# A transformer block on one core: when the output projection's operand and weights are loaded beside attention

## The chip, the cores and the metric

The kernel runs on one core of a Trainium2 chip. A core has TensorE (PE, matrix products; its weight loads are listed as PEld), VectorE (DVE), ScalarE (ACT), GpSimd (POOL) and SyncE (SP), which here only issues DMA transfers. The metric is the time on the device of one execution, in microseconds; lower is better.

## The reference

One block with adaptive layer norm, for 2 sequences of 1024 tokens with 1024 features. Shifts, scales and gates come from a product of `silu(c)` with `wmod`.

```python
h = _layernorm(x) * (1 + ca) + sa
qkv = clip(h @ Wqkv.T, -8, 8)                      # q and k get a layer norm of their own
scores = q k^T * scale + slope_h * (key - query)   # 32 heads of 32, causal
out = softmax(scores) @ v
x = x + ga * (out @ Wout.T)
h = _layernorm(x) * (1 + cb) + sb
x = x + gb * (((silu(h @ Wg.T * ag)) * (h @ Wu.T * au)) @ Wd.T * ad)   # inner size 2752
```

## The kernel before

**Seven products.** Every large product is done in 2 x 2 blocks by a scheme with seven block products and sums of blocks. `SEVEN` (L780) lists them in order, with the index `e` from 0 to 6:

| e | product | left operand | weights |
|---|---|---|---|
| 0 | P1 | A11 | B11 |
| 1 | P2 | A12 | B21 |
| 2 | U2 | S2 | T2 |
| 3 | P5 | S1 | T1 |
| 4 | U3 | S3 | T3 |
| 5 | P53 | S4 | B22 |
| 6 | U6 | A22 | T4 |

A11, A12, A21 and A22 are blocks of the left operand, S1 to S4 their sums (S1 = A21 + A22, S2 = S1 - A11, S3 = A11 - A21, S4 = A12 - S2). B are blocks of the weights and T sums of them, which an earlier part of the kernel has computed and stored. One product is four matmul instructions; the trace has two records for each.

**Attention in groups.** Attention goes through 32 groups `GROUPS` (L1044): batch `b`, half `qb` of the queries, and `k`, four heads. Groups 0 to 15 are batch 0, 16 to 31 batch 1. Each has 4 (`qb` = 0) or 8 (`qb` = 1) units, one for each block of 128 keys. `chunk` (L1056) loads a group's queries `cq`, keys `ck` and values `cv` on SP's queue; there are two buffers of each, so `cq` and `ck` wait until TensorE has done with the scores of the group two before and `cv` until it has done with that group's product with the values (`weigh`, L1113). `scores` makes the scores `sc`, ScalarE their exponentials `p`, GpSimd masks them, VectorE and GpSimd add them up for the row sums. At the end of a group `weigh` stores the result `ao` (L1130), and `settle` (L1137) the row sums `sum` (L1154); after the last group of a half the reciprocals `rec` are stored.

**Dense work beside it.** `together` (L1198) runs attention as one generator and the dense work as another and decides by estimated times which one records its next instructions. TensorE's order is that recorded order (`pinned`). The other queues, SP's among them, are ordered by a scheduler, subject to the dependencies that the kernel adds by `behind` (an instruction stands after another one in the queue). While attention of batch 1 runs, the dense work is the output projection, `output` (L1318), for the blocks (b, j) of 256 tokens: (0,0) to (0,3), (1,0), (1,1), and after the end of attention (1,2) and (1,3).

**The operand.** `operand` (L1260) makes the left operand of one block in steps, each ending in a `yield`. Step 1 issues eight loads on SP: four `rb` (the reciprocals of the row sums, each row spread over 32 partitions, L1268) and the four blocks A11, A12, A22, A21 (`aoA<-ao`, L1284). Step 2 multiplies A22 and A21 by `rb`, step 3 A11 and A12 and makes S1, step 4 makes S2 and S3, step 5 makes S4. A11, A22, S1 and S2 are made on VectorE, A12, A21, S3 and S4 on GpSimd. `ahead` (L1342), called between the products of one block, starts the next block's operand at `e` = 2 and takes one more step at each of `e` = 3, 4, 5 and 6:

```python
if e == 2 and nxt not in made and not step and (nxt[0], 2 * nxt[1] * P // QB) in settled:
    step[0], step[1] = operand(*nxt, ap_), e
    next(step[0])
elif e > 2 and step and e > step[1]:
```

**The output weights.** `weights_b` (L800) loads B11 and B21 at once; the five others, T2, T1, T3, B22 and T4 (`wT_o`, `wB_o`), are put in the list `later`, and `ahead` issues them two products before their use: `while later and 7 - len(later) <= e + 2`.

**After a block.** Each product's bank is evicted by ScalarE or VectorE (`oP`, `oU`), gated and added to `xr` on GpSimd, normalised, transposed by TensorE (L751), evicted by VectorE as `h2t` (L871), summed into `tT` and stored as `hs` for the feed-forward stage, which follows after about 1350 us. All transposes and the row sums of `settle` use one and the same bank, so a transpose waits for the `h2t` evictions of the one before.

Of the kernel before, what the change touches and what calls it, by code (L numbers as in the profile page):

```python
# [19 lines left out]
P = 128  # L20
H = 32
HD = 32
# [458 lines left out]
def kernel(  # L481
# [19 lines left out]
    nc = tc.nc  # L501
# [183 lines left out]
    def behind(ins, first):  # L685

        tc.add_manual_dep(
            ins.ins, first.ins.name,
            mybir.DependencyInfo(mybir.DependencyClass.NoSync, mybir.DependencyReason.DATA),
            reason="behind",  # L690
        )

    last_exp = [None]
    last_chunk = [None]
    chain_copy = [None]
    last_mask = [None]
    beside = [False]

    def masked(ins):
        if beside[0]:  # L700
            behind(ins, last_mask[0])
        return ins
# [344 lines left out]
    def attention(pools, adders, banks):  # L1047
# [8 lines left out]
        def chunk(i):  # L1056
            if i < len(GROUPS) and i not in chunks:
                b, qb, k = GROUPS[i]
                while (b, qb) not in ready:
                    yield None  # L1060
                n = (qb + 1) * QB
                qc = chp.tile([P, QB], FP, tag="cq", name=f"cq_{b}_{i}")
                kc = chp.tile([P, S], FP, tag="ck", name=f"ck_{b}_{i}")
                vc = chp.tile([P, NT, P], FP, tag="cv", name=f"cv_{b}_{i}")
                nc.sync.dma_start(qc, qk_dram[b][0][:, k, ds(qb * QB, QB)])
                nc.sync.dma_start(kc[:, 0:n], qk_dram[b][1][:, k, 0:n])
                last_chunk[0] = nc.sync.dma_start(vc[:, 0 : n // P], v_dram[b][:, 0 : n // P, ts(k, P)])
                chunks[b, qb, k] = chunks[i] = (qc, kc, vc)

        def scores(b, qb, k, jb):  # L1070
            qc, kc, _ = chunks[b, qb, k]
# [106 lines left out]
        for i, u in enumerate(UNITS + [None] * (LAG + 2)):  # L1178
# [10 lines left out]
            if i >= LAG and queue:  # L1189
                b, qb, k, jb, ps = queue.pop(0)  # L1190
# [69 lines left out]
    def operand(b, j, ap_):  # L1260


        qb, y0 = 2 * j * P // QB, 2 * j * P % QB
        at, low_, rbp = ap_
        rb = rbp.tile([P, KC, 2 * P], FP, tag="rb", name=f"rb_{b}_{j}")
        nk = KC - 1 if (b, qb, KC - 1) == GROUPS[-1] else KC
        for g in range(4):
            nc.sync.dma_start(  # L1268
                rb[ts(g, HD), 0:nk],
                rec_dram[b][qb].rearrange("(k g) q -> g k q", g=4)[g][0:nk, ds(y0, 2 * P)].partition_broadcast(HD),  # L1270
            )
        if nk < KC:
            nc.scalar.copy(rb[:, nk], right["last"][:, ds(y0, 2 * P)])
        a = {
            q: (low_ if q in ("A22", "S1", "S2", "S4") else at).tile(
                [P, KC // 2, P], FP, tag=q, name=f"ao{q}_{b}_{j}", bufs=2 if q in ("A21", "A22") else None,
            )
            for q in ("A11", "A12", "A21", "A22", "S1", "S2", "S4")
        }
        blocks = (  # L1280
            (0, 0, "A11", nc.vector), (0, 1, "A12", nc.gpsimd), (1, 1, "A22", nc.vector), (1, 0, "A21", nc.gpsimd),
        )
        for m, kh, q, eng in blocks:
            nc.sync.dma_start(a[q], ao_dram[b][qb][:, ds(kh * 4, 4), ds(y0 + m * P, P)])  # L1284
        yield

        def scaled(q):
            m, kh, eng = next((m, kh, eng) for m, kh, q_, eng in blocks if q_ == q)
            ins = eng.tensor_mul(a[q], a[q], rb[:, ds(kh * 4, 4), ts(m, P)])
            if eng is nc.gpsimd:  # L1290
                masked(ins)

        scaled("A22")
        scaled("A21")
        yield
        scaled("A11")
        nc.vector.tensor_add(a["S1"], a["A21"], a["A22"])
        scaled("A12")
        yield
        nc.vector.tensor_sub(a["S2"], a["S1"], a["A11"])  # L1300
        a["S3"] = a["A21"]
        masked(nc.gpsimd.tensor_sub(a["S3"], a["A11"], a["A21"]))
        yield
        masked(nc.gpsimd.tensor_sub(a["S4"], a["A12"], a["S2"]))
        made[b, j] = a
        yield

    def operands(b, j, *args):
# [5 lines left out]
    gates = {}  # L1314

    later = []

    def output(b, js, pools, banks, bt, todo, keep, q0=3, after=None):  # L1318

# [8 lines left out]
        for j in js:  # L1328
# [5 lines left out]
            for m in range(2):  # L1334
                xr = tkp[j % 2].tile([P, D], FP, tag="xr", name=f"xr_{b}_{qts[m]}")
                nc.sync.dma_start(xr, x[b, ts(qts[m], P), :])
                xs.append(xr)
            part_t = {}
            step = {}
            nxt = (b, j + 1) if j + 1 < NJ else (b + 1, 0)  # L1340

            def ahead(e):  # L1342


                while later and 7 - len(later) <= e + 2:
                    later.pop(0)()
                if e == 2 and nxt not in made and not step and (nxt[0], 2 * nxt[1] * P // QB) in settled:
                    step[0], step[1] = operand(*nxt, ap_), e
                    next(step[0])
                elif e > 2 and step and e > step[1]:  # L1350
                    step[1] = e
                    next(step[0])

            def read(q, bank):
                if q in ("P1", "U2", "P5"):
# [313 lines left out]
    if True:  # L1669
# [180 lines left out]
        with ExitStack() as dn:  # L1850
# [22 lines left out]
            def load(dst, src):  # L1873
                ins = nc.sync.dma_start(dst, src)
                if loads:
                    behind(ins, loads[-1])
                loads.append(ins)
# [141 lines left out]
```

## Time and profile before

| | us |
|---|---|
| median of 3 runs | 2265.51 |
| the 3 runs | 2265.51, 2263.86, 2270.93 |
| profiled execution | 2262.51 |
| its span, first to last instruction | 2260.7 |
| TensorE busy in it | 2143.8 |
| mean granted TensorE clock | 0.984 |

All rows of the profile are from that one execution, with times in microseconds from the start of the span. A row of the timeline gives start, duration, engine, line, operation, output <- inputs and shape, with equal instructions that follow each other merged; the brackets give the idle time of the engine before it and what ended it. Names have no buffer numbers: `aoA` is any of the blocks A, `aoS` any sum, `wT_o` any of the output weights T. A row of the waits gives who waited for whom, then total, number of times and longest. `SPq` is SP's queue: its rows are the issue of transfers, not their course. The profile gives no landing time of transfers; where a landing is named, it is the time at which a wait for it ended.

### The profile page before, as it was taken

The page shows a single profiled execution, that of the slowest core. Times are in us where ns is not written, and L with a number is a line of the kernel's source. Part 1 is how long each engine was busy: PE and PEld are TensorE (multiplying, and loading weights), DVE is VectorE, ACT ScalarE, POOL GpSimd, SP SyncE. Part 2 cuts the span into 40 slices and gives each one's busy share as a digit, 9 for nine tenths or more (in the row PEclk, how much of TensorE's full clock was granted, in tenths as well). Part 3 has the DMA queues.
Part 4 walks back from the last instruction along what each step waited for, and adds up shares of the span by engine and source line. Part 5 has one row for each costly group of instructions (what it writes and reads, how often), then busy time and mean ns, then how long its engine had stood idle before and what let it go on. Part 6 is the DMA issues. An engine that isn't in the chain of part 4 may idle for free. (4 is left out here: it accounts for less than half of the span.)

```text
span 2260.7 us, 27238 instructions
## 1 busy us (share of the span) xinstructions
PE 2143.8 (95%) x9537; PEld 1170.8 (52%) x9537; DVE 1352.1 (60%) x1811; ACT 943.3 (42%) x1782; POOL 1098.0 (49%) x775
## 2 busy tenths in 40 slices
PE   5999999999999999899999888899998999999998
PEld 2444444333333333232222235788877888788887
DVE  5775653455566633457667676788976555534535
ACT  1222223445444445466555414554554444333331
POOL 2330112443344554586677563677977667312212
PEclk9999999999999999999999999999999999999999
DMA  9877776545425531854553366767758777598765
GB/s 370 321 288 265 293 276 240 184 145 194 168 80 199 174 116 48 281 171 140 148 168 103 100 204 205 216 206 245 251 195 256 242 228 233 202 379 314 275 225 189
DMA packets 319349, 482.44 MB, mean 213 GB/s; under 512 B 16092, under 2 KB 235036, under 8 KB 310244
## 3 DMA queue, kind: packets, MB, share of 16 engines
q1 hardware_dynamic: 316752, 472.19, 62.4%
q10 hardware_dynamic: 2452, 8.43, 1.0%
q8 instruction: 77, 1.26, 0.2%
q14 instruction: 68, 0.56, 0.1%
HBM read 323.01 MB, written 157.55 MB: 213 GB/s over the span
## 5 line engine op out<-in xcount | busy, mean ns | idle before, releaser
L1103 ACT ACTIVATE p<-sc,kw 128x128 f32<-128x128 f32 (+3 forms) x1024 | 422.1, 513 | 390.1 <-PE sc L748 365.5
L748 PE MATMUL bank<-wT,a 128*128 128x512 f32 x768 | 366.6, 611 | 14.1 <-DVE wT L834 7.9
L1135 POOL TENSOR_TENSOR p<-p,p 128x1024 f32<-128x1024 f32 (+3 forms) x128 | 263.4, 2058 | 212.8 <-PE av L748 186.0
L1135 DVE TENSOR_TENSOR p<-p,p 128x1024 f32<-128x1024 f32 (+3 forms) x192 | 242.7, 1281 | 110.8 <-POOL p L1107 68.2
L748 PE MATMUL bank<-wB,a 128*128 128x512 f32 x576 | 270.2, 605 | 1.2 <-DVE raw L993 0.6
L748 PEld LDWEIGHTS bank<-wT,a 128*128 128x128 f32 x768 | 136.8, 191 | 200.2 <-issue 167.1
L1107 POOL TENSOR_SCALAR_AFFINE_SELECT p<-p 128x256 f32<-128x256 f32 x256 | 137.1, 548 | 182.3 <-ACT p L1103 171.3
L748 PE MATMUL sc<-cq,ck 32*128 32x512 f32 (+3 forms) x1536 | 181.6, 538 | 11.7 <-DMA ck<-qk 8.4
L748 PE MATMUL av<-p,cv 128*32 128x512 f32 (+3 forms) x1536 | 168.8, 500 | 13.2 <-POOL p L1107 13.0
L748 PEld LDWEIGHTS bank<-wB,a 128*128 128x128 f32 x576 | 102.1, 189 | 141.9 <-issue 128.8
L1899 DVE TENSOR_TENSOR lo<-lo,hi 128x1408 fp32r<-128x1408 f32 x56 | 96.3, 1723 | 93.1 <-ACT hi L1898 93.1
L748 PEld LDWEIGHTS sc<-cq,ck 32*128 32x128 f32 x1536 | 61.8, 184 | 149.8 <-issue 82.4
L1898 ACT CAST hi<-lo 128x1408 fp32r<-128x1408 f32 x56 | 76.9, 1375 | 134.0 <-DMA lo<-act 89.7
L1963 POOL TENSOR_TENSOR early_P<-early_P,x1in 128x512 f32<-128x512 f32 x16 | 35.7, 2234 | 165.1 <-DVE early_P L1961 160.3
L748 PEld LDWEIGHTS av<-p,cv 128*32 128x32 f32 x1536 | 33.7, 108 | 146.5 <-issue 80.9
L1694 POOL TENSOR_TENSOR wS<-wst,wst 128x1024 fp32r<-128x1024 f32 (+1 forms) x22 | 65.9, 2997 | 87.5 <-PE uy L748 61.9
L993 DVE TENSOR_TENSOR raw<-P,bank 128x512 f32<-128x512 f32 x48 | 32.8, 684 | 119.1 <-PE bank L748 98.9
L748 PE MATMUL gx<-hs,wS 128*128 128x512 f32 (+1 forms) x352 | 90.6, 399 | 10.6 <-ACT gP L1808 7.0
L748 PE MATMUL gy<-hs,wS 128*128 128x512 f32 (+1 forms) x352 | 89.4, 396 | 9.5 <-DVE gP L1813 6.4
L748 PE MATMUL gx<-hs,wA 128*128 128x512 f32 (+1 forms) x352 | 89.0, 393 | 1.5 <-ACT h2t L873 1.5
L748 PE MATMUL uy<-hs,wS 128*128 128x512 f32 (+1 forms) x352 | 87.2, 390 | 1.2 <-DVE uP L1813 1.2
L748 PE MATMUL ux<-hs,wS 128*128 128x512 f32 (+1 forms) x352 | 88.3, 393 | 0.0
(266 smaller groups left out, 3996.3 us busy)
## 6 DMA issues: line engine op xcount, KB each, us to landing
lo<-act SPq DMA_DIRECT2D x56, 704.0 KB
a<-hop SPq DMA_DIRECT2D x20, 1792.0 KB
wm<-in_L_wmod_dram SPq DMA_DIRECT2D x48, 512.0 KB
act<-aS SPq DMA_DIRECT2D x88, 256.0 KB
wB<-in_L_attn_Wqkv_dram SPq DMA_DIRECT2D x21, 1024.0 KB
wst<-in_L_ffn_Wg_dram SPq DMA_DIRECT2D x40, 512.0 KB
wst<-in_L_ffn_Wu_dram SPq DMA_DIRECT2D x40, 512.0 KB
qk<-qs SPq DMA_DIRECT2D x16, 1024.0 KB
```

Of the source, the lines that this page charges most:

```text
L748: return in_order(nc.tensor.matmul(*args, **kw_))
L993: nc.vector.tensor_add(dst, part_t[MATE[q]], bank)
L1103: last_exp[0] = nc.scalar.activation(p[:, g, lo:hi], sp[:, g, lo:hi], AF.Exp, bias=kw[:, d, h_ : h_ + 1])
L1107: last_mask[0] = nc.gpsimd.affine_select(out=p[:, :, 0:P], in_=p[:, :, 0:P], pattern=[[0, 2], [1, P]], compare_op=ALU.is_ge, fill=0.0, bas ...
L1135: adders[b](half, jb).tensor_add(dst, dst, ps[half][:, :, 0:n])
L1694: ins = nc.gpsimd.tensor_add(f["S1"], raw["A21"], raw["A22"])
L1898: nc.scalar.copy(hi, lo.bitcast(FP))
L1899: nc.vector.tensor_sub(lo, lo.bitcast(FP), hi.bitcast(FP))
L1963: eng.tensor_add(y, y, x1_of.pop(s))
```

## The change

The eight loads of an operand are no longer issued at once but put in a list `deferred`; `flush()` issues them. It is called in `chunk` right behind a group's `cq`, `ck` and `cv`, and at the latest when `operand` goes on to its second step. While attention runs, each of these loads is put behind the last `cv` in SP's order; for the first operand (0,0), and once attention is over, they are issued at once. `chunk` also issues one of the remaining output weights, and `ahead` issues them one product before their use instead of two. The second step of `operand` is taken at `e` = 4 instead of 3 and each later one a product later; the last (S4) is taken at the start of the next block, from the list `unfinished`, and `made` is set one step earlier so that the next block finds its operand.

```diff
@@ -692,6 +692,11 @@
 
     last_exp = [None]
     last_chunk = [None]
+    deferred = []
+
+    def flush():
+        while deferred:
+            deferred.pop(0)()
     chain_copy = [None]
     last_mask = [None]
     beside = [False]
@@ -1066,6 +1071,9 @@
                 nc.sync.dma_start(kc[:, 0:n], qk_dram[b][1][:, k, 0:n])
                 last_chunk[0] = nc.sync.dma_start(vc[:, 0 : n // P], v_dram[b][:, 0 : n // P, ts(k, P)])
                 chunks[b, qb, k] = chunks[i] = (qc, kc, vc)
+                flush()
+                if later:
+                    later.pop(0)()
 
         def scores(b, qb, k, jb):
             qc, kc, _ = chunks[b, qb, k]
@@ -1264,11 +1272,6 @@
         at, low_, rbp = ap_
         rb = rbp.tile([P, KC, 2 * P], FP, tag="rb", name=f"rb_{b}_{j}")
         nk = KC - 1 if (b, qb, KC - 1) == GROUPS[-1] else KC
-        for g in range(4):
-            nc.sync.dma_start(
-                rb[ts(g, HD), 0:nk],
-                rec_dram[b][qb].rearrange("(k g) q -> g k q", g=4)[g][0:nk, ds(y0, 2 * P)].partition_broadcast(HD),
-            )
         if nk < KC:
             nc.scalar.copy(rb[:, nk], right["last"][:, ds(y0, 2 * P)])
         a = {
@@ -1280,9 +1283,25 @@
         blocks = (
             (0, 0, "A11", nc.vector), (0, 1, "A12", nc.gpsimd), (1, 1, "A22", nc.vector), (1, 0, "A21", nc.gpsimd),
         )
+
+        def load(*args):
+            ins = nc.sync.dma_start(*args)
+            if beside[0] and (b, j) != (0, 0):
+                behind(ins, last_chunk[0])
+
+        for g in range(4):
+            deferred.append(lambda g=g: load(
+                rb[ts(g, HD), 0:nk],
+                rec_dram[b][qb].rearrange("(k g) q -> g k q", g=4)[g][0:nk, ds(y0, 2 * P)].partition_broadcast(HD),
+            ))
         for m, kh, q, eng in blocks:
-            nc.sync.dma_start(a[q], ao_dram[b][qb][:, ds(kh * 4, 4), ds(y0 + m * P, P)])
+            deferred.append(
+                lambda m=m, kh=kh, q=q: load(a[q], ao_dram[b][qb][:, ds(kh * 4, 4), ds(y0 + m * P, P)])
+            )
+        if (b, j) == (0, 0) or not beside[0]:
+            flush()
         yield
+        flush()
 
         def scaled(q):
             m, kh, eng = next((m, kh, eng) for m, kh, q_, eng in blocks if q_ == q)
@@ -1300,9 +1319,9 @@
         nc.vector.tensor_sub(a["S2"], a["S1"], a["A11"])
         a["S3"] = a["A21"]
         masked(nc.gpsimd.tensor_sub(a["S3"], a["A11"], a["A21"]))
+        made[b, j] = a
         yield
         masked(nc.gpsimd.tensor_sub(a["S4"], a["A12"], a["S2"]))
-        made[b, j] = a
         yield
 
     def operands(b, j, *args):
@@ -1314,6 +1333,7 @@
     gates = {}
 
     later = []
+    unfinished = []
 
     def output(b, js, pools, banks, bt, todo, keep, q0=3, after=None):
 
@@ -1336,20 +1356,25 @@
                 nc.sync.dma_start(xr, x[b, ts(qts[m], P), :])
                 xs.append(xr)
             part_t = {}
+            for go in unfinished:
+                next(go)
+            unfinished.clear()
             step = {}
             nxt = (b, j + 1) if j + 1 < NJ else (b + 1, 0)
 
             def ahead(e):
 
 
-                while later and 7 - len(later) <= e + 2:
+                while later and 7 - len(later) <= e + 1:
                     later.pop(0)()
                 if e == 2 and nxt not in made and not step and (nxt[0], 2 * nxt[1] * P // QB) in settled:
                     step[0], step[1] = operand(*nxt, ap_), e
                     next(step[0])
-                elif e > 2 and step and e > step[1]:
+                elif e > 3 and step and e > step[1]:
                     step[1] = e
                     next(step[0])
+                    if e == 6:
+                        unfinished.append(step[0])
 
             def read(q, bank):
                 if q in ("P1", "U2", "P5"):
```

## The prediction

> **What bounds the kernel now.** I read the page first: TensorE is busy 95% of the span, so only its idle microseconds, and those at a lowered clock, can be won.
>
> ```profile
> PE 2143.8 (95%) x9537; PEld 1170.8 (52%) x9537; DVE 1352.1 (60%) x1811; ACT 943.3 (42%) x1782; POOL 1098.0 (49%) x775
> ```
>
> The change touches the stretch in which attention of batch 1 runs beside the output projection, about 915 to 1310. The waits of TensorE (here between 900 and 1345) name one large loss:
>
> ```profile
> PE av L748 <- POOL p L1107: 13.0, 8, 5.7
> PE bank L751 <- DVE h2t L871: 11.2, 9, 3.8
> PE sc L748 <- DMA ck<-qk: 8.4, 1, 8.4
> ```
>
> The stretches around it show TensorE fully idle for six microseconds and then granted half its clock:
>
> ```profile
> 934.00:940.00 6.00, 5.10 (x43) 1.50 (x42) 4.11 (x4) 3.19 (x9) 5.10 (x8) 1.00 1.11 221
> 940.00:946.00 6.00, 0.00 (x0) 0.00 (x0) 3.37 (x5) 0.00 (x0) 1.84 (x2) 0.79 1.13 293
> 946.00:952.00 6.00, 4.46 (x11) 1.72 (x12) 0.12 (x1) 2.35 (x4) 1.01 (x2) 0.50 1.03 373
> ```
>
> (Columns: length; busy PE, PEld, DVE, ACT, POOL; granted clock; DMA share; GB/s.) The timeline of SP's queue says why the keys came late: they were issued at 941.85, behind three output weights and seven transfers of the next operand.
>
> ```profile
> 920.25 0.44 SPq L820 DMA_DIRECT2D wT_o<-wt  x1
> 920.79 1.42 SPq L1130 DMA_DIRECT2D ao<-aot  x1
> 922.31 0.54 SPq L1067 DMA_DIRECT2D cv<-v  x1
> ...
> 923.73 1.94 SPq L820 DMA_DIRECT2D wT_o<-wt  x2
> 926.86 4.65 SPq L1268 DMA_DIRECT2D rb<-rec  x4
> 932.05 6.43 SPq L1284 DMA_DIRECT2D aoA<-ao  x3
> 938.96 2.30 SPq L1130 DMA_DIRECT2D ao<-aot  x1
> 941.31 0.49 SPq L1065 DMA_DIRECT2D cq<-qk  x1
> 941.85 0.50 SPq L1066 DMA_DIRECT2D ck<-qk  x1
> ```
>
> TensorE's timeline shows what follows: scores, then product P5, then U3 at 957.17.
>
> ```profile
> 947.54 2.09 PE L748 MATMUL sc<-cq,ck 32*128 32x512 f32 x8 [8.44 <-DMA ck<-qk]
> 949.56 3.78 PE L748 MATMUL bank<-wT_o,aoS 128*128 128x512 f32 x4
> 954.90 1.98 PE L748 MATMUL bank<-wT_o,aoS 128*128 128x512 f32 x4
> 957.17 1.13 PE L748 MATMUL bank<-wT_o,aoA 128*128 128x512 f32 x2
> ```
>
> **What goes.** In the built program of the changed kernel TensorE's order is the same, and cq and ck of group 19 stand before the operand, right behind T1. The 8.44 us wait goes. So does the slow clock after it: the four matmul records took 3.78 instead of 1.98 (1.80), the scores held TensorE 2.02 to the next start instead of 1.07 at 926.44 (0.95), the next values' product 0.77 instead of 0.57 (0.20). Together 8.44 + 2.95 = 11.39. By the Trainium skill (TensorE: Matmul & The Clock Gate, Part 1) an idle window of about 3.4 us halves the clock until about as long has been busy; half speed for 3.4 us would cost 1.7, the gain be 10.1. The row decides: 11.4. Without any wait U3 would start at 957.17 - 11.39 = 945.8.
>
> **What is late next: T2 and T3.** T2 stood before ao and cv of 18, now behind both. T3 stood before the operand, now behind cq, ck, two xr tiles, cv and ao of the next group and all eight operand transfers (the eighth, A21, was issued near 459 before, since nothing held it). When a transfer landed can be read where the queue itself or VectorE waits for it: second xr 928.0, T2 930.5, ao 931.2, cv 932.0, T1 by 935.0, T3 938.9, A11 943.9, A12 944.7, A22 945.4, keys 947.5. They land in the order of issue. I take from these gaps 0.7 per 256 KB (0.65 per xr half), 2.5 for T2, about 3.2 for T3 (between 2.5 and its gap of 3.9), and 4.2 for the four rb. Replayed in the new order from 928.0: ao, cv and T2 give 928.0 + 1.5 + 2.5 = 932.0, where TensorE asks at 930.93: 1.1 us of wait. T1 has the same bytes before it as now, 935.0, in time. cq and ck 936.4, needed near 940: the cure works. Two xr 939.0, cv and ao 940.4, four rb 944.6, four A 947.5, T3 950.7. TensorE asks for T3 at 945.8 + 1.1 = 946.9: 3.8 us of wait. After the 3.26 us wait at 1325.69 four records took 3.68 instead of 1.98, so 1.7 more. B22 and T4 follow behind ao, cq, ck and cv at about 956.4 and 959.2; before, P53 started 10.3 after U3, so it asks near 961 or later, T4 later still: nothing.
>
> Sum here: 11.39 - 1.1 - 3.8 - 1.7 = 4.8 us won.
>
> A rule speaks against that replay: by the Trainium skill (DMA: Bandwidth & Descriptors, Queues, rings and completion order) completion is not in order per issuing engine; a later small transfer may be complete first. If T3 passed the operand, its wait and slow clock would go and the gain be 10.3. The ten landings above are in order, so I keep 4.8 and use the other as a bound. The lower bound: T3 is issued once the first rb has landed (eight semaphores are used in turn), at 941.5 to 943.5; with its issue-to-landing of before, 938.9 - 925.4 = 13.5, it lands at 955 to 957, and next to nothing is won.
>
> **The other operands.** Loads of (0,2), (0,3), (1,0), (1,1) now start behind cv of groups 24, 26, 28 and 30 and one ao, near 1009, 1075, 1141 and 1202 on the old time axis. Eight transfers need about 7 us by the paces above, 12 at worst. Their first products start at 1039, 1100, 1171 and 1246, and their sums stand on VectorE near 1023, 1089, 1155 and 1218: at least 4 us are left. On SP they delay the group's row sums, the xr and hs transfers and the next cq and ck. The sums' single rs buffer is wanted a group later (12 to 30 us); ck of group 25, issued at 1013.46, is first used at 1062; nothing reads hs before the feed-forward stage. Nothing, then.
>
> **Moved sums, on VectorE and GpSimd.** No operation is added; four on VectorE (0.69 each) and four on GpSimd (1.27 each) per operand stand later. Where they leave, these waits shrink:
>
> ```profile
> 1021.30 0.66 PE L751 MATMUL bank<-ident,xr 128*128 128x128 f32 x4 [1.83 <-DVE h2t L871]
> 1060.48 1.12 PE L748 MATMUL bank<-wT_o,aoS 128*128 128x512 f32 x2 [2.35 <-DVE oP L1365]
> ```
>
> At 1021.30 the evictions h2t stood behind S1 and S2 (1.21 + 0.69), which go: 1.8 won. At 1060.48 oP waited behind A11 of (0,3), which itself waited 1.41 for its load: about 1.75 won. Where they arrive: for (1,0), A11 and A22 now stand among the h2t evictions that the transpose at 1157.02 waits for, 2 x 0.69 = 1.4 lost. For (1,1), A22, A11, S1 and S2 stand before an h2t that ended at 1223.24, where TensorE asks at 1224.41: 2.8 more, less 0.6 and the 1.2 of slack, and a little handed on to the 3.8 us wait at 1232.55, about 1.4 lost. For (0,3) the h2t behind them is the last of its tile, and the GpSimd masks delayed by 2.6 end near 1092 for a product at 1096.7: nothing. S4 moves to the start of the next output and is used five products later: nothing. (1,2) and (1,3) load at once as before; of (1,3) the sums slip behind one tT operation of 0.7 us, ten before their use. Net 3.55 - 2.8 = 0.75 won; both ends, none of the gains or none of the losses, are -2.8 and +3.6.
>
> **Sum.** 4.8 + 0.75 = 5.55 us. The profiled execution took 2262.51 (span 2260.7 and 1.8 around it), so it becomes 2257.0. It lies 3.0 below the median 2265.51; the same difference on the median's scale gives 2260.0, or 0.24% less. About 0.3% (6.8 us) is what can be told from no change.
>
> **Rivals.**
> - *Fully hidden.* T2 and T3 are in time: 11.4 + 0.75 = 12.1, 2253.4. For it: low traffic once the keys are out of the way, and transfers need not land in order. Against it: eight operand transfers stand directly before T3. Chance 0.22.
> - *The wait changes hands.* T3 lands at 955 to 957: U3 starts where it did, with a slow clock again; between 2 won and 4 lost, near 2266. For it: T3's 13.5 us before. Chance 0.17.
> - *Slower.* One mechanism: T3, issued at 943.5 behind eight loads at the 221 GB/s that the stretch from 934 shows while they run, lands after 961, since the 1 MB of T3 then shares with wB22 and T4 issued behind it. Landing at 964 costs 964 - 957.2 = 6.8 and 1.7 of clock above now, 2274. It decides from 957.2 upward and beats the measurement's grain from about 962. Against it: T3's bytes stand ahead of theirs. Chance 0.17, the reordered evictions going worse included.
> - *It does not do what it says.* If the keys still waited, the time would stay; the new order excludes that.
>
> **How the numbers follow.** My forecast, 2 to 8 us won, has 0.44. Faster by over 0.3%: the hidden case, 0.22, and 0.14 of the forecast's upper part, 0.36. Same: the rest of the forecast, 0.30, and the wait that changes hands, 0.17, 0.47. Slower: 0.17. The range leaves out 2 in 10: it goes down past the hidden case with all VectorE gains (11.4 + 3.6 = 15.0, 2250.5), to 2251, and up to 2271, the losses on VectorE on top of the wait that changes hands.
>
> **What would show it.** After the change no wait sc <- DMA ck near 940; clock near 1.00 there; a wait of bank<-wT_o for DMA wT_o near 947 of 3 to 4 us; T2's near 931 about 1. The waits at 1021 and 1060 are gone, those near 1157 and 1224 longer by 1.4 and 1.7. Wrong if T3 shows no wait, or one over 9 us, or if cq and ck of a later group are waited for.

## The result, and the profile after

The changed kernel takes 2272.98 us (median of 20 runs, 2263.89 to 2278.61), the kernel before, timed with it, 2263.47. The ratio is 1.0042, 95% interval 1.0033 to 1.0050: 0.42% slower, about 9.5 us. The forecast was 2260.0 with a range up to 2271. From here on every version is given by its ratio to the kernel before, each compared with runs of that kernel on the same chip; "+9.5" is (ratio - 1) x 2263. By the intervals a difference between two such numbers is uncertain by about 3 us.

The profiled execution after took 2272.35 (span 2270.5). TensorE has the same instructions, and 2.5 us more busy time; so most of what was lost is idle time. The page of the changed kernel:

```profile
PE 2146.3 (95%) x9537; PEld 1172.4 (52%) x9537; DVE 1359.2 (60%) x1811; ACT 943.3 (42%) x1782; POOL 1104.8 (49%) x775
```

The largest of its waits of TensorE between 900 and 1345, to be set against those before (lines lie five to 25 further down in the file):

```profile
PE av L753 <- POOL p L1115: 14.8, 9, 4.8
PE bank L756 <- DVE h2t L876: 13.4, 8, 4.2
PE bank L753 <- DMA wT_o<-wt: 8.9, 2, 5.5
PE bank L753 <- DVE oP L1390: 4.7, 2, 3.2
```

The 8.4 us for the keys are gone. In their place stand two waits for output weights, 8.9 together, and the waits for GpSimd's `p` and VectorE's `h2t` are 1.8 and 2.2 longer. The stretches around the old wait (length; busy PE, PEld, DVE, ACT, POOL; granted clock; DMA share; GB/s):

```profile
928.00:934.00 6.00, 2.81 (x20) 0.78 (x18) 3.04 (x4) 3.84 (x8) 5.78 (x8) 1.00 1.01 407
934.00:940.00 6.00, 5.79 (x26) 2.03 (x30) 0.69 (x1) 0.58 (x1) 1.21 (x3) 0.72 0.45 171
940.00:946.00 6.00, 6.00 (x44) 1.83 (x37) 4.47 (x4) 4.04 (x11) 4.66 (x6) 1.00 0.87 204
946.00:952.00 6.00, 4.80 (x31) 1.57 (x29) 1.74 (x3) 4.54 (x9) 2.64 (x5) 1.00 0.99 235
952.00:958.00 6.00, 1.69 (x2) 0.50 (x2) 0.69 (x1) 0.00 (x0) 0.00 (x0) 0.73 1.03 373
```

The hole at 940 is now two holes, at 930 and 952, each with a lowered clock behind it. Look at the DMA share of the second row as well: from 934 to 940, a few us before T3 is wanted, the transfer engines are less than half used. SP's timeline says why:

```profile
921.50 1.32 SPq L825 DMA_DIRECT2D wT_o<-wt  x1
...
923.54 0.58 SPq L825 DMA_DIRECT2D wT_o<-wt  x1
926.11 0.32 SPq L1070 DMA_DIRECT2D cq<-qk  x1
927.28 0.32 SPq L1071 DMA_DIRECT2D ck<-qk  x1
928.55 1.05 SPq L1356 DMA_DIRECT2D xr<-_attn_hidden_states_dram  x2
938.27 0.38 SPq L1072 DMA_DIRECT2D cv<-v  x1
938.93 0.33 SPq L1138 DMA_DIRECT2D ao<-aot  x1
939.35 2.09 SPq L1288 DMA_DIRECT2D rb<-rec  x4
941.54 5.64 SPq L1288 DMA_DIRECT2D aoA<-ao  x4
947.23 2.93 SPq L825 DMA_DIRECT2D wT_o<-wt  x1
```

T2 is issued at 921.50, T1 at 923.54, then the keys of group 19. After the second `xr` the queue stands for 8.7 us (928.55 + 1.05 to 938.27) in front of `cv` of group 19, which needs the buffer that TensorE frees with the last product of group 17 with its values. That product stands behind U2, and U2 waits for T2. TensorE's timeline:

```profile
934.21 3.65 PE L753 MATMUL bank<-wT_o,aoS 128*128 128x512 f32 x4 [3.40 <-DMA wT_o<-wt]
937.79 0.43 PE L753 MATMUL av<-p,cv 128*32 128x128 f32 x8
...
943.97 1.14 PE L753 MATMUL sc<-cq,ck 32*128 32x512 f32 x8
...
956.31 2.07 PE L753 MATMUL bank<-wT_o,aoA 128*128 128x512 f32 x2 [5.51 <-DMA wT_o<-wt]
```

U2 starts 3.28 us later than before (930.93), its four records take 3.65 at the lowered clock, and the product with the values ends at 938.2: then SP goes on. The scores of group 19 start at 943.97 without a wait, 3.57 earlier than before in spite of that. Matched instruction by instruction, TensorE is 0.2 us ahead of the kernel before at 925, 4.9 behind at 937.8, 6.4 ahead at 948, and after T3's wait and slow clock 1.6 behind at 962. The whole gain is gone there.

The rest is lost between 1100 and 1245, at three places, one for each of the operands (0,3), (1,0) and (1,1):

```profile
1101.84 1.85 PE L753 MATMUL av<-p,cv 128*32 128x384 f32 x8 [3.12 <-POOL p L1115]
...
1162.63 0.83 PE L756 MATMUL bank<-ident,xr 128*128 128x128 f32 x4 [4.19 <-DVE h2t L876]
...
1233.42 0.66 PE L756 MATMUL bank<-ident,xr 128*128 128x128 f32 x4 [1.34 <-DVE h2t L876]
```

Before, there was no wait at the first and third of these, and one of 0.61 at the second. The kernel before at the first two:

```profile
1099.17 0.85 PE L748 MATMUL av<-p,cv 128*32 128x384 f32 x8
...
1157.02 0.66 PE L751 MATMUL bank<-ident,xr 128*128 128x128 f32 x4 [0.61 <-DVE h2t L871]
```

At the first place TensorE waits for the last masks on GpSimd. They stand behind the output's work (`tT`, `oU`, `xr`), as they did before, where they were done at 1098.99, 0.2 ahead of their product:

```profile
1098.22 0.77 POOL L1107 TENSOR_SCALAR_AFFINE_SELECT p<-p 128x256 f32<-128x256 f32 x2
```

Now that work starts later. A12 and A21 of (0,3) stand in front of it on GpSimd, and even then GpSimd is idle for 1.38 until `h2t` is evicted, because on VectorE A11, A22 and S1 of the same operand (0.88, 1.43 and 0.68, from 1089.41 on) stand among the evictions:

```profile
1087.00 1.94 POOL L1308 TENSOR_TENSOR aoA<-aoA,rb 128x512 f32<-128x512 f32 x1 [0.27 <-DMA sum<-rs]
...
1089.72 1.69 POOL L1308 TENSOR_TENSOR aoA<-aoA,rb 128x512 f32<-128x512 f32 x1
...
1093.61 1.27 POOL L1241 TENSOR_TENSOR tT<-h2t 128x512 f32<-128x512 f32 x1 [1.38 <-DVE h2t L876]
...
1098.20 2.24 POOL L1242 TENSOR_TENSOR tT<-h2t,tT 128x512 f32<-128x512 f32 x1
1100.40 1.75 POOL L1115 TENSOR_SCALAR_AFFINE_SELECT p<-p 128x256 f32<-128x256 f32 x2
```

VectorE's timeline ahead of the second: A11 and A22 of (1,0) stand among the evictions, as the prediction had it, but they take 2.21 and 1.52, not 0.69 each.

```profile
1157.64 2.21 DVE L1308 TENSOR_TENSOR aoA<-aoA,rb 128x512 f32<-128x512 f32 x1
1159.77 1.04 DVE L876 TENSOR_SCALAR h2t<-bank,modt 128x128 f32<-128x128 f32 x3
1160.73 1.52 DVE L1308 TENSOR_TENSOR aoA<-aoA,rb 128x512 f32<-128x512 f32 x1
1162.17 0.40 DVE L876 TENSOR_SCALAR h2t<-bank,modt 128x128 f32<-128x128 f32 x1
```

By the shifts of TensorE against the kernel before, instruction by instruction, it is 0.7 ahead at 1080. The first place costs 5.0 (2.3 of it comes back by 1131), the second 4.4 and the third 2.4, slow clocks and smaller waits nearby included; at 1246 it is 8.9 behind.

### The profile page after: what moved, and what is told of

Read it like the earlier page. It is cut to its first block, busy times and chain, and to the rows that moved or that the text cites. A ratio compares the mean times of both kernels' runs of the same rounds, so it can differ in the third digit from the quotient of the medians.

```text
span 2270.5 us, 27209 instructions
## 1 busy us (share of the span) xinstructions
PE 2146.3 (95%) x9537; PEld 1172.4 (52%) x9537; DVE 1359.2 (60%) x1811; ACT 943.3 (42%) x1782; POOL 1104.8 (49%) x775
## 5 line engine op out<-in xcount | busy, mean ns | idle before, releaser
L1143 DVE TENSOR_TENSOR p<-p,p 128x1024 f32<-128x1024 f32 (+3 forms) x192 | 248.1, 1308 | 114.5 <-POOL p L1115 66.8
L753 PE MATMUL ux<-hs,wA 128*128 128x512 f32 (+1 forms) x352 | 87.6, 390 | 0.5 <-DVE uP L1838 0.5
```

What stands on the lines that cost most here:

```text
L753: return in_order(nc.tensor.matmul(*args, **kw_))
L1143: adders[b](half, jb).tensor_add(dst, dst, ps[half][:, :, 0:n])
```

## The experiments

Theory A says that two of the three parts lose and one wins: the late weights (W) lose because of T2's and T3's place on SP's queue, the late sums (S) because they crowd VectorE and GpSimd where evictions and masks are due, and the late loads (L) win. The rivals: the transfers ask for more than the engines can move, whatever their order (B); the late loads, not the late sums, push the operand's work into the evictions (C); gains are given back later anyway (D). In the expectations the letters are those of each text.

In every kernel below TensorE's order is the same. Profiled executions differ by up to 4 us before the stretch is reached, so places are judged by their waits and by shifts within a trace.

### One part undone, or one alone

*W undone* (no_w):

```diff
-                if later:
-                    later.pop(0)()
...
-                while later and 7 - len(later) <= e + 1:
+                while later and 7 - len(later) <= e + 2:
```

> The changed kernel with its weights issued two products ahead again (T2 in front of the stores, T3 in front of group 19's queries and keys); the loads behind the group and the later sums stay. Theory A (two separate losses: T2 and T3 come late because of where they now stand on SP's queue, and the operand's multiplications and sums crowd the evictions later on): the waits for wT_o near 931 and 951 and the slow clock behind them go, so that TensorE runs about 11 us ahead of the kernel before at 960, instead of 1 us behind; the crowding stays, about 9 to 10 us lost between 1090 and 1245. Time near 2261.5 (2258 to 2265). Rival B (T3 is late because eight operand loads and everything else share the DMA bandwidth, not because of its place): a wait for wT_o of 3 us or more stays near 950, time 2268 or more.

Measured: 1.0032 (1.0020 to 1.0045), +7.2: 2.3 less than the changed kernel. The weights' waits went as theory A had it (one of 1.6 is left, T2's), but the time did not: it lies where rival B had it, for another reason. TensorE was 11 us ahead at 953, and 3.7 ahead at 965, because the keys of the next group, 20, were late instead (times of the kernel before). SP's timeline of this kernel, and TensorE's wait:

```profile
948.00 1.37 SPq L821 DMA_DIRECT2D wB_o<-in_L_attn_Wout_dram  x1
949.47 0.66 SPq L1136 DMA_DIRECT2D ao<-aot  x1
950.23 1.28 SPq L1070 DMA_DIRECT2D cq<-qk  x1
951.56 0.44 SPq L1071 DMA_DIRECT2D ck<-qk  x1
```

```profile
957.48 2.09 PE L753 MATMUL sc<-cq,ck 32*128 32x512 f32 x8 [5.49 <-DMA ck<-qk]
```

The wait moved one group on: the keys of group 20 stand behind the eight operand loads and behind B22, again two products ahead. Neither theory had this.

*S undone* (no_s):

```diff
-                elif e > 3 and step and e > step[1]:
+                elif e > 2 and step and e > step[1]:
                     step[1] = e
                     next(step[0])
-                    if e == 6:
-                        unfinished.append(step[0])
```

(and `made` is set after S4 again).

> The changed kernel with the sums at their old products (steps at e = 3, 4, 5, 6; S4 in the same block); late loads and late weights stay. Theory A (the later sums crowd the evictions): the waits of TensorE for p near 1102, for h2t near 1162 and 1241 return to the sizes they had before (none, 0.6, below 4), the waits at 1021 and 1060 return; 7 to 9 us less than the changed kernel, time near 2265. Rival C (it is the late loads that hold the operand's multiplications back until the evictions are due, wherever the sums are recorded): the multiplications stand among the h2t evictions all the same, and the time stays within 3 us of 2273.

Measured: 1.0001 (0.9992 to 1.0010), +0.2. Theory A holds: 9.3 less than the changed kernel, somewhat more than it said. TensorE's waits of 3.12 and 4.19 at the two places are gone, though on VectorE the operand's multiplications still stand later than before. Rival C falls.

*L alone, of one operand* (l01): W and S undone, and the loads put off for (0,1) only.

```diff
-        if (b, j) == (0, 0) or not beside[0]:
+        if (b, j) != (0, 1):
             flush()
```

> The kernel before with one thing of the change: the eight loads of operand (0,1) alone are issued behind group 19's queries, keys and values. Weights, sums and all other operands' loads as before. Theory A: the 8.44 us wait for the keys and its slow clock go, nothing takes their place, nothing is crowded later: 10 to 12 us less than the kernel before, 2252 (2250 to 2256). Rival B (the transfers share the bandwidth and the wait only changes hands, to an operand block or T3): less than 4 us won, 2260 or more. Rival D (what is won in one place is given back at the next wait for an engine that is itself late): 4 to 8 us won, 2256 to 2260.

Measured: 0.9977 (0.9968 to 0.9986), -5.2: half of what theory A gave, and in rival D's stretch of times, but not for its reason. It is once more the keys of group 20:

```profile
PE sc L753 <- DMA ck<-qk: 4.6, 1, 4.6
```

*S alone* (only_s): L and W undone.

> The kernel before with the later sums alone (steps at e = 4, 5, 6, S4 at the start of the next block); loads and weights as before. Theory A (the later sums crowd the evictions): 5 to 9 us more than the kernel before, 2269 to 2272, with the waits near 1102, 1162 and 1241 as in the changed kernel. Rival C (the late loads hold the multiplications back, not the later sums): within 3 us of the kernel before, 2261 to 2266, and a gain at 1021 of about 1.5 us to be seen.

Measured: 1.0034 (1.0024 to 1.0044), +7.7. The sums lose nearly the whole 9.5 by themselves, with no late load about. But the waits are not where theory A put them (the first two are 0.8 and 0.6); 3.7 are lost at 1187 to 1199, where the changed kernel loses nothing. The cause of these shows below, where the sums are split. It is not that of the changed kernel, so that the two losses are nearly alike in size is in part chance.

*L alone, of all operands* (only_l): W and S undone.

> The kernel before with the late loads alone, for every operand beside attention; weights two products ahead and sums at their old products. If the late loads of (0,2) to (1,1) cost nothing, as the prediction had it, this equals the kernel with (0,1) alone: 2259 (2257 to 2261). If they hold the multiplications back into the evictions, it is 3 us or more above that, 2262 or more. Set against the kernel with late loads and late weights (2264.0), it gives what the late weights cost: 5 us by the theory that T2 and T3 come late in their new places, nothing by the rival that their place makes no difference.

Measured: 0.9983 (0.9973 to 0.9992), -3.8. Within its interval that is the kernel with (0,1) alone: the late loads of (0,2) to (1,1) cost nothing that shows. Against the kernel with L and W (+0.2) the late weights cost 4.0 in this company.

### Which operands' sums

The sums were put off only for some operands: for (0,1) and (0,2) on top of the kernel before (s12), for (0,3), (1,0) and (1,1) on top of it (s345), and the reverse on top of the changed kernel: back at their old products for those three (a345), for (1,0) alone (a10), for (0,3) alone (a03). The edit is one condition each, here that of a10:

```diff
-                elif e > 3 and step and e > step[1]:
+                elif e > (3 if nxt not in ((1, 0),) else 2) and step and e > step[1]:
```

> The kernel before with the sums of operands (0,1) and (0,2) one product later, loads, weights and the other sums as before. The later sums of all five cost 7 us. Theory A (they cost where a long group's softmax and the output's evictions already fill VectorE and GpSimd, from 1090 on; for these two the moves only take work out of the way of the evictions at 1021 and 1060): 1 to 3 us less than the kernel before, 2261 to 2263. Rival (every operand's later sums cost alike, about 1.4 us each): 2266 to 2267.

Measured: 1.0004 (0.9993 to 1.0015), +0.9. No cost, and no gain either, where 1 to 3 won were expected; the wait at 1021 is 2.8, longer than before.

> The kernel before with the sums of operands (0,3), (1,0) and (1,1) one product later, the rest as before: the other half of the later sums. Theory A: all the cost is here, 7 to 10 us more than the kernel before, 2271 to 2274. Rival (alike for every operand): about 4 us, 2267 to 2268.

Measured: 1.0025 (1.0017 to 1.0034), +5.7. The two halves add to 6.6, against 7.7 for all. Most of the cost is in these three; it lies between the theory's 7 to 10 and the rival's 4. VectorE's timeline shows a mechanism that no theory had:

```profile
1191.76 0.69 DVE L1304 TENSOR_TENSOR aoA<-aoA,rb 128x512 f32<-128x512 f32 x1 [5.62 <-DMA aoA<-ao]
```

VectorE stands still for 5.62 us in front of A22 of (1,1), whose load is not there. There is one buffer for `rb`: the first `rb` of (1,1) was issued at 1161.29, when A12 of (1,0), now late on GpSimd, had ended at 1161.27 (before: 1139.34 and 1139.31). The softmax additions behind A22 wait with it, and TensorE at 1195 for the exponentials. With the loads late as well, as in the changed kernel, that particular stall is not there and the crowding is.

> The changed kernel with the sums of (0,3), (1,0) and (1,1) at their old products; everything else as changed (loads late, weights late, sums of the other operands late). Theory A (what the later sums cost in the changed kernel is at these three, where the evictions and the long groups' masks fall together with them): the waits for p near 1102 and for h2t near 1162 return to what they were before; 8 to 9 us less than the changed kernel, 2264 to 2265. Rival (once the loads are late, the early operands' sums cost too): 2267 or more.

Measured: 1.0006 (0.9993 to 1.0020), +1.4: 8.1 less than the changed kernel. Theory A holds; what is left for the early operands' sums, 1.2 (+1.4 against +0.2), is within the intervals.

> The changed kernel with the sums of (1,0) alone at their old products. By the shifts between the two traces the late sums of (1,0) cost 4 us at the transpose near 1162; theory A: that wait falls from 4.2 back to about 0.6 and A11 and A22 take 0.7 to 0.9 each instead of 2.21 and 1.52; 3 to 5 us less than the changed kernel, 2268 to 2270. Rival (what is won here is taken back by the wait at 1241, because VectorE and GpSimd are behind anyway): 2271 or more, and the wait near 1241 longer than 3.8.

Measured: 1.0018 (1.0007 to 1.0029), +4.1: 5.4 less. The wait of 4.19 is 0.60 again, and the wait near 1241 is 3.84, not longer. A11 and A22 of (1,0) stand among softmax additions at 1133, away from the evictions.

> The changed kernel with the sums of (0,3) alone at their old products. By the shifts they cost about 4 us at the product with the values near 1102, which waits for a mask behind A12 and A21 on GpSimd, of which 1.4 comes back by 1128. Theory A: that wait falls from 3.1 to about 0.8; 2 to 4 us less than the changed kernel, 2269 to 2271. Rival (it comes back later anyway): within 1.5 us of the changed kernel.

Measured: 1.0016 (1.0006 to 1.0025), +3.6: 5.9 less, more than the 2 to 4 expected. The wait of 3.12 near 1102 is gone altogether; that of (1,0) is still there, 4.19. The two single steps add to more than the 8.1 of all three; the intervals (2 to 3 us to each side) allow it, and the exact shares stay open.

### VectorE or GpSimd

The changed kernel, but for these three operands the multiplications of one engine handle a quarter of the columns (short_v: A11 and A22 on VectorE; short_g: A12 and A21 on GpSimd), at the same place in the queue. The two blocks are loaded from `x` instead of `ao` and not multiplied by `rb`, so this part of the output projection is not computed. Of the edit for short_v, the part on the multiplication:

```diff
-            ins = eng.tensor_mul(a[q], a[q], rb[:, ds(kh * 4, 4), ts(m, P)])
+            n = 1 if eng is nc.vector and (b, j) in ((0, 3), (1, 0), (1, 1)) else 4
+            by = rb[:, ds(kh * 4, 4), ts(m, P)] if n == 4 else a[q][:, 0:n]
+            ins = eng.tensor_mul(a[q][:, 0:n], a[q][:, 0:n], by)
```

> The changed kernel, with the multiplications of A11 and A22 of (0,3), (1,0) and (1,1) on VectorE cut to a quarter (128 of 512 columns, by another factor; these blocks are loaded from x instead of the attention's result so that the values stay in range: this part of the product is not computed). Their place in the queue, the sums and GpSimd's part stay. If the losses come from VectorE's work between the h2t evictions, the wait near 1162 falls from 4.2 to 2 or less and the time by 3 to 5 us, 2268 to 2270; if they come from GpSimd being behind with its masks, the time stays within 2 us of the changed kernel and the wait for p near 1102 stays.

Measured: 1.0025 (1.0016 to 1.0034), +5.7: 3.8 less.

> The same for GpSimd: the multiplications of A12 and A21 of (0,3), (1,0) and (1,1) are cut to a quarter in the same way (that part of the product is not computed); VectorE's part stays. If GpSimd being behind with the masks is what costs, the wait for p near 1102 (3.1) goes below 1, VectorE's A11 and A22 of (1,0) shrink only where they overlap these two, and the time falls by 3 to 6 us, 2267 to 2270. If it is VectorE's own work, the time stays within 2 us of the changed kernel and the wait near 1162 stays at about 4.

Measured: 1.0008 (0.9999 to 1.0017), +1.8: 7.7 less. TensorE's two places with VectorE's part cut:

```profile
1099.57 1.39 PE L753 MATMUL av<-p,cv 128*32 128x384 f32 x8 [3.84 <-POOL p L1115]
...
1158.84 1.11 PE L756 MATMUL bank<-ident,xr 128*128 128x128 f32 x4 [2.34 <-DVE h2t L876]
```

and with GpSimd's part cut, and VectorE's timeline of that kernel:

```profile
1101.95 1.85 PE L753 MATMUL av<-p,cv 128*32 128x384 f32 x8 [1.75 <-POOL p L1115]
...
1162.06 0.66 PE L756 MATMUL bank<-ident,xr 128*128 128x128 f32 x4 [3.35 <-DVE h2t L876]
```

```profile
1157.91 2.22 DVE L1315 TENSOR_TENSOR aoA<-aoA,rb 128x512 f32<-128x512 f32 x1
1160.05 1.04 DVE L876 TENSOR_SCALAR h2t<-bank,modt 128x128 f32<-128x128 f32 x3
1161.01 0.68 DVE L1315 TENSOR_TENSOR aoA<-aoA,rb 128x512 f32<-128x512 f32 x1
```

It is both; by the times GpSimd's part counts for more. In these traces neither wait goes: cutting VectorE's part brings the wait for `h2t` from 4.19 to 2.34, cutting GpSimd's to 3.35. For the masks the start of TensorE's product is the fairer measure, since it came to that place at other times in each trace. Against the kernel before, and less the shift at 1080, the product is 3.4 late in the changed kernel, 2.5 with VectorE's part cut and 2.0 with GpSimd's; the fall of the wait for `p` below 1 that was expected of short_g did not come (1.75). What is left may be the operand's sums, which neither cut touches; that was not tried. Nor does the trace of short_g show where the 7.7 are won: it is of the slowest of its 22 runs (2272.68), and loses 7.1 from 1080 to 1246, against 9.6 in the changed kernel.

Shortening GpSimd's operations brings VectorE's A22 from 1.52 to 0.68, although nothing about A22 was changed. A11 keeps its 2.22: beside it GpSimd adds up `p`, in this kernel too.

### T3 in another place

The changed kernel, with each output weight issued in front of a group's values (t3first), so T3 stands right behind group 19's keys and not behind the operand:

```diff
+                if later:
+                    later.pop(0)()
                 last_chunk[0] = nc.sync.dma_start(vc[:, 0 : n // P], v_dram[b][:, 0 : n // P, ts(k, P)])
                 chunks[b, qb, k] = chunks[i] = (qc, kc, vc)
                 flush()
-                if later:
-                    later.pop(0)()
```

> The changed kernel with one thing moved: each later output weight is issued in front of a group's values instead of behind the operand's loads, so T3 stands right behind group 19's keys, T2 in front of the values of group 18; operand loads, sums and all else as changed. Theory A (T3 was late by 5.5 us and T2 by 3.4 because of what stood in front of them): no wait for an output weight over 1.5 us; but the keys of group 20 then wait about 5 us behind the operand's loads, as they did in both kernels with T3 in its old place; 2 to 3 us less than the changed kernel, 2270 to 2271. Rival (the place makes the whole difference and nothing takes the wait over): 2262 to 2264.

Measured: 1.0014 (1.0005 to 1.0024), +3.2: 6.3 less than the changed kernel, more than the 2 to 3 of theory A. No weight is waited for, so the place does make T2's and T3's waits. The keys of group 20 are waited for less than the 5 us expected:

```profile
956.91 1.14 PE L753 MATMUL sc<-cq,ck 32*128 32x512 f32 x8 [0.94 <-DMA ck<-qk]
```

But in this execution TensorE reached the stretch 3 us later than in the kernel before (at 925), and so asked later for them. They came at nearly the same moment in every kernel with (0,1)'s loads behind group 19: their scores started at 957.48 (no_w), 957.60 (l01), 958.12 (only_l), 956.91 here. So 0.94 is not a size to rely on, and the next kernel shows what it is. The rival that the place makes the whole difference has the place right and the time wrong, since the late sums are still in.

### Both losing parts put right, and a version of its own

The changed kernel with the weights in front of the values and S undone (t3nos):

> The changed kernel with both of its losing parts put right: the later weights in front of a group's values (T3 right behind group 19's keys), and the sums at their old products; the late loads stay. If the parts add up as measured so far (late loads won about 4 of 11 because the keys of group 20 took the wait over; the weights in front of the values took neither wait; the sums at their old products cost nothing), TensorE is 9 to 11 us ahead of the kernel before at 1021 and the time is 2253 to 2257, like the kernel with (0,1)'s loads behind group 20. If the late loads of the other operands cost with the sums at their old products, 2258 or more.

Measured: 0.9964 (0.9952 to 0.9977), -8.1, as expected (2255.4 on the scale of 2263.5). With these two parts put right nothing of the loss is left. TensorE was 7 us ahead at 1021, not 9 to 11. In the stretches where before and after had their holes:

```profile
934.00:940.00 6.00, 6.00 (x56) 1.90 (x48) 3.23 (x3) 3.78 (x10) 4.19 (x7) 1.00 1.02 396
940.00:946.00 6.00, 6.00 (x32) 2.12 (x32) 2.99 (x4) 3.91 (x8) 4.05 (x6) 1.00 1.15 204
946.00:952.00 6.00, 6.00 (x49) 1.95 (x52) 0.69 (x1) 4.20 (x12) 0.45 (x2) 1.00 1.14 265
```

A smaller hole is left behind them, the keys of group 20 once more:

```profile
956.39 1.96 PE L753 MATMUL sc<-cq,ck 32*128 32x512 f32 x8 [3.83 <-DMA ck<-qk]
```

B22 stands behind these keys here and in front of them in no_w (5.49) and l01 (4.55), which leaves most of the wait to the operand's loads; B22's place was not tried by itself.

The other way, from the kernel before: only the loads of (0,1) are moved, behind the keys of group 20, whose products come long before (0,1)'s first at 979; the sums of (0,1) and (0,2) are a product later (l20), or those of (0,1) alone (l20b).

```diff
-                nc.sync.dma_start(kc[:, 0:n], qk_dram[b][1][:, k, 0:n])
+                last_chunk[0] = nc.sync.dma_start(kc[:, 0:n], qk_dram[b][1][:, k, 0:n])
+                if i == 20:
+                    flush()
```

> Built on what the first runs showed: with operand (0,1) alone behind group 19's queries and keys, the wait moved to the keys of group 20 (4.6 us at 957.6, and a slow clock after it). Here the eight loads of (0,1) stand one group later, behind the keys of group 20, with weights two products ahead as before; the sums of (0,1) and (0,2) are taken one product later, all others as before. Theory A (the keys wait because operand transfers with time to spare stand in front of them; the first product of (0,1) starts only at 979): neither group 19 nor group 20 waits for keys, no output weight is waited for, and TensorE is 10 to 12 us ahead of the kernel before at 980; time 2250 to 2254. Rival B (from 920 to 960 the transfers together ask for more than the engines can move, whatever their order): a wait of 3 us or more for keys, an output weight or the operand shows between 940 and 985, and the time is 2257 or more.

Measured: 0.9956 (0.9942 to 0.9971), -10.0. Rival B falls: the transfers do fit, in this order. Of the waits for keys between 900 and 1000 this is left:

```profile
PE sc L753 <- DMA ck<-qk: 0.4, 1, 0.4
```

> The kernel with operand (0,1)'s loads behind the keys of group 20, now with the sums of (0,1) alone one product later; (0,2)'s are back at their old products. The later sums of (0,1) and (0,2) together measured 1 us slower than before, within the interval. If (0,2)'s are the part that costs, 1 to 2 us less, 2253; if neither does, the same 2254 to 2255.

Measured: 0.9961 (0.9946 to 0.9977), -8.8: the same. l20, l20b and t3nos beat both kernels and cannot be told from each other.

The account, from the parts: late loads with the weights well placed -8.1 (t3nos); the later weights in their changed places, T2 and T3 above all, +8.3 (no_s less t3nos); late sums +9.3 (the changed kernel less no_s). That these add to +9.5 is arithmetic, each being the difference to the one before. The split depends on what else is in the kernel: late weights count 8.3 here but 4.0 from only_l to no_s, because in only_l the keys of group 20 wait 5.8, and in no_s they do not wait.

## Why the prediction was wrong, step by step

- **The keys' wait and its slow clock, 11.39 won: right.** From 937.8 to 948.5 TensorE goes from 4.9 behind to 6.4 ahead, 11.4: the row, not the 10.1 worked out from the page's rule.
- **T2, 1.1 late: mis-sized.** The wait is 3.40, and four records behind it took 3.65 instead of 1.98. The replay put T2's landing at 932.0; it came at 934.2, 12.7 us after its issue; why it took 2.2 longer than in the replay is not shown. The slow clock was charged to T3's wait and not to this one.
- **T3, 3.8 late: mis-sized, by the step "two xr 939.0, cv and ao 940.4".** The replay let the queue run and counted bytes only. In fact it stood in front of `cv`, until a product of TensorE that was itself behind the wait for T2; with that the transfer engines ran at a share of 0.45. T3 was issued at 947.23 and landed at 956.3, where 950.7 was forecast. Net at this place: 4.8 won predicted, 1.8 lost measured (0.2 ahead at 925, 1.6 behind at 962). The rival in which the wait changes hands had T3 at 955 to 957 and between 2 won and 4 lost: it is what happened here, but its landing time was right by luck: it had T3 issued at 941.5 to 943.5 and 13.5 on the way, where it was issued some 4 to 6 later and took 9.1.
- **T3 passing the operand: did not happen.** T3 landed at 956.3. The last of the operand loads, A21, was in by 954.20: T4, issued then, had to wait for it (the eighth transfer before, by the order of semaphores that the prediction names). So the 10.3 were not to be had; the rule as the prediction gives it speaks of a small transfer, and T3 is four times as large as an operand load.
- **B22 and T4, nothing: right.** No wait for them shows. What the prediction named as a sign but did not price is a wait for the keys of a later group. Those of group 20 were late in all five kernels in which T3 was in time and (0,1) stood behind group 19, by 4 to 6 us in four and 0.9 in t3first: even with T2 and T3 in time the rival "fully hidden" was not to be had in full.
- **The other operands' late loads, nothing: right** within 2 us (only_l against l01), and t3nos has them all.
- **The moved sums where they leave, 3.55 won: not theirs.** In the changed kernel the wait at 1021 goes, and with it a slow clock behind it that the prediction did not count, 3.5 together; a new wait of 1.7 for the row sums (`rs`) near 1039 takes 1.9 back; the wait at 1060 falls from 2.35 to 1.52, 0.8. Net 2.4. But only_l, where no sum is moved, wins 3.4 at 1021 and 2.4 at 1060 as well, and put off alone the sums of (0,1) and (0,2) won nothing (s12): what is won there comes with the late loads.
- **The moved sums where they arrive, 2.8 lost, bounds +3.6 to -2.8: the step that failed most.** Measured 9.3 for all the moved sums, where 0.75 won was forecast. For (1,0), 1.4 was counted as two times 0.69, the time of such an operation with no GpSimd arithmetic beside it; among the evictions they took 3.73. For (0,3), "the GpSimd masks delayed by 2.6 end near 1092" looked at the masks of one product. The next ones, for the product at 1099.17, had 0.2 to spare behind the output's work on GpSimd; that work waited for the later evictions, and these masks ended at 1102.15. The bound was built from the same short durations, so it was none. The trace of before held the warning: one of these sums took 2.85 there (S1 of (1,1), at 1212).
- **The chance of slower, 0.17, rested on T3 landing after 961.** It landed at 956.3. The slower case came from the sums, which the prediction mentioned in half a sentence and did not price.

## What to carry to other kernels

When transfers are put in a new order on one queue, replay the queue's own waits, not only the bytes: ask of every transfer that needs a buffer who frees it, and whether that engine will itself be waiting for something in the same queue. An operation that is moved costs what it costs beside its new neighbours; take the contended duration from the trace, and look at what moves back behind it on both engines. If a change bundles several moves, price each as if it stood alone: here one was worth 8 to 10 us, and the two that came with it took it all back and as much again.

## What the runs showed of the hardware

- An operation of VectorE with both inputs in SBUF can slow down beside GpSimd's arithmetic. Of the operand's operations on VectorE (128x512, f32) in the changed kernel between 900 and 1345, nine had no tensor-tensor operation of GpSimd beside them and took 0.68 to 0.89; twenty had one for over half of their time and took 0.68 to 2.29, seven of them over 1.5 and six under 0.8. The additions `oP` and `oU` of the same size, with one input in PSUM, took 0.62 to 0.69, with GpSimd beside them (11) or without (14). The Trainium skill (SBUF — State Buffer, Who interferes with whom) states this: an instruction of VectorE with two SBUF inputs contends with a GpSimd instruction that reads SBUF, one with at most one SBUF input, outside the two-port modes, does not. That short_g brought A22 from 1.52 to 0.68 agrees.
- A wait of 3.40 us lowered the clock (four records in 3.65 instead of 1.98), but so did one of 1.83, at 1021 in the kernel before: what came next took 1.6 more, the scores 2.09 instead of 1.14. The wait of 2.35 at 1060 cost nothing beyond itself. By the records of the granted clock in the traces it was half from 943.49 to 953.73 and from 1022.00 to 1025.41 before, and from 934.28 to 937.69 and from 954.76 to 961.58 after. These stretches are one, two or three times 3.41 long, and within a trace their ends lie on one grid of 3.41. So the length of a wait alone does not give its price here.
- Transfers of 1 MB on one queue took 9.1 (T3) and 12.7 us (T2) from issue to the end of the wait for them, with the share of the transfer engines at 0.99 to 1.03 for T3 and 0.99 to 1.01 for T2.
